# A graph-attention kernel: the four-head aggregation in four 32-column tiles of TensorE instead of two of 64

## The chip, the cores and the metric

The kernel runs on one core of one Trainium2 chip. The metric is the device time of one execution, in microseconds (us). The kernel before took 2711.55 us, the median of two runs (2709.53 and 2713.56 us). The profile that is read here is of one execution whose span is 2711.9 us.

## The reference

Four layers of graph attention follow one another on 16 independent graphs of 1024 nodes with 256 features each. All graphs share one 1024 x 1024 adjacency matrix, which is thin and symmetric and has ones on its diagonal. Layers 0 and 2 have four heads of 64 features, layers 1 and 3 one head of 256. Cut to its core, a layer is:

```python
h = relu(layernorm(x))                       # per node, over 256 features
Wh = h @ W                                   # (1024, 256) @ (256, 256), split into H heads of D
e = leaky_relu(a_src . Wh_i + a_dst . Wh_j)  # one number for each pair (i, j) and head
alpha = softmax over j of e, where adj[i, j] is set
x = x + elu(alpha @ Wh)                      # layer 3: relu in place of elu
```

All of it is in float32. The large piece of arithmetic is `alpha @ Wh`: for each of the 64 pairs of graph and layer, a 1024 x 1024 matrix of weights for each head, times the projected features.

## The kernel before

The kernel computes unnormalised weights, `w[j, i] = max(grow[i], rcol[j]) * mask[j, i]`, with source nodes j on the partitions and target nodes i along the free dimension, and folds the remaining factor into the projected features `whx`. An extra column of `whx` carries the denominator of the softmax, so a four-head product has 64 + 1 = 65 columns and a one-head product 256 + 1 = 257. There are 8 blocks of 128 nodes (`C = 8`).

```python
def weights(n, h, jc):                       # VectorE: one tile of weights, 128 sources x 1024 targets
    w = state[n]["w", h, jc] = work.tile([P, N], F32, name="w", bufs=WBUFS)       # WBUFS = 18
    nc.vector.scalar_tensor_tensor(w, state[n]["g", h], state[n]["rcol"][:, jc, h:h + 1],
                                   masks[...][:, jc, :], op0=ALU.max, op1=ALU.mult)

def aggregate(n, h, i0, per):                # TensorE: per blocks of 128 targets, from block i0 on
    H = LAYERS[steps[n][1]][0]
    D = F // H
    st = state[n]
    ...
    acc = ps_acc.tile([P, per, D + 1], F32, name="acc")                           # 2 buffers
    cols = P // 2 if H > 1 else P
    for q in range(per):
        for jc in range(C):

            for o in range((i0 + q) * P, (i0 + q + 1) * P, cols):
                nc.tensor.matmul(acc[o % P:o % P + cols, q, :],
                                 lhsT=st["w", h, jc][:, o:o + cols],
                                 rhs=st["whx"][:, jc, h, :], start=(jc == 0),
                                 stop=(jc == C - 1))
    nc.scalar.activation(st["y"][:, i0:i0 + per, h, :], acc, AF.Copy)
```

In `aggregate` the weights `w` are the stationary operand (they are loaded into the array) and `whx` is the moving one (it streams through). A four-head layer calls it with `per = 4` (two groups for each head, so 32 x 4 x 2 = 256 groups), a one-head layer with `per = 1`. With `cols = 64` each block of 128 targets is made by two matmuls: targets 0 to 63 go to the left half of the array's columns and to partitions 0 to 63 of `acc`, targets 64 to 127 to the right half and to partitions 64 to 127. The sum over the eight `jc` is accumulated in PSUM.

The two other users of TensorE that matter are the projection (`pw`, line 233: the transposed features times `wx`) and the transposes ahead of it (line 221). The program interleaves pieces of the preparation of later steps between the groups of `aggregate`; the order is fixed when the program is built.

Of the kernel before, what the change touches and what calls it, by code (L numbers as in the profile page):

```python
# [32 lines left out]
P = 128  # L33
# [24 lines left out]
def kernel(ctx: ExitStack, tc: tile.TileContext, x, adj, ws, avs, out):  # L58
# [234 lines left out]
    def aggregate(n, h, i0, per):  # L293
# [3 lines that stand above are left out]
        if h == 0 and i0 == 0:  # L297
            st["y"] = work.tile([P, C, H, D + 1], F32, name="y")
        acc = ps_acc.tile([P, per, D + 1], F32, name="acc")
        cols = P // 2 if H > 1 else P  # L300
        for q in range(per):
            for jc in range(C):

# [6 lines that stand above are left out]
# [128 lines left out]
    with tc.manual_schedule():  # L438
# [50 lines left out]
        for n in range(len(steps)):  # L489
            for k, (h, i0, per) in enumerate(groups(n)):  # L490
                while planned < len(steps) and agenda_of[planned][0] <= 8 * n + k:
                    plan(planned)
                    planned += 1
                emit_tiles(place[n, h, C - 1] + 1, must=True)
                aggregate(n, h, i0, per)
                if i0 + per == C:
                    done["free"] = place[n, h, C - 1] + 1
                while ending and ending[0][0] <= k:
                    ending.pop(0)[1]()
                if 8 * n + k in later:  # L500
                    later[8 * n + k]()
                prepare(8 * n + k)
                ahead = 6 if per > 1 else 3
                emit_tiles(min(done["tiles"] + ahead, done["free"] + WBUFS))
            for _, piece in ending:
                piece()
            ending = finish(n)
# [35 lines left out]
```

## Time and profile before

| What | Value |
|---|---|
| time | 2711.55 us (2709.53 to 2713.56) |
| span of the profiled execution | 2711.9 us |
| TensorE matmuls busy | 2567.2 us, 95% of the span, 40080 records |
| TensorE weight loads busy | 2269.2 us, 84%, 40080 records |
| VectorE busy | 1900.3 us, 70% |
| ScalarE busy | 1229.6 us, 45% |
| GpSimd busy | 992.3 us, 37% |
| mean granted TensorE clock | 0.984 of full speed |

"PE" is TensorE's matmuls, "PEld" its weight loads, DVE is VectorE, ACT is ScalarE, POOL is GpSimd. A line such as L305 is the line of the kernel that issued the instruction. Matmuls are pipelined, and the end of one is modelled in the profile: the duration of a record holds the latency of the array, and many records overlap. So the busy share of PE says that it nearly always had something in flight, and not how near it is to its limit. How fast a stretch of matmuls goes is read from starts: the time of an unbroken stretch divided by the number of records in it.

Every float32 matmul of `aggregate` and of the projection stands in the trace as two records, each with a weight load of its own: the program's 16384 four-head matmuls are 32768 records. The built program holds, for each such matmul, a weight load and a matmul and then once more a weight load and a matmul, on the same tile of the array. They are called its two passes here.

### The profile page before, as it was taken

The numbers are of one execution on the slowest core, as the hardware profiler recorded it, in microseconds if no ns is written. First come the engines' busy times: TensorE is split into PE (matmuls) and PEld (weight loads), VectorE is DVE, ScalarE is ACT, GpSimd is POOL, SyncE is SP. The second block draws the span as 40 slices with busy tenths as digits, with TensorE's granted clock in tenths as the row PEclk, the third lists the DMA queues.
The fourth block names the chain that finished last, engine by engine and source line by source line (L and its number), as shares of the span: only waits on it lengthen the run. The fifth ranks groups of instructions, "written<-read, shape, count | busy, mean of one in ns | idle before, by whom it ended". The sixth has DMA issues, their size and how long they took to land.

```text
span 2711.9 us, 89498 instructions
## 1 busy us (share of the span) xinstructions
PE 2567.2 (95%) x40080; PEld 2269.2 (84%) x40080; DVE 1900.3 (70%) x2041; ACT 1229.6 (45%) x3337; POOL 992.3 (37%) x1242
## 2 busy tenths in 40 slices
PE   3799999999999999999999999999999999999998
PEld 2688888888888888888888888888888888788876
DVE  3796686477875688666876778748687567678752
ACT  3344445444354554544444454544435444444431
POOL 2133424423424534344242353442332443443321
PEclk9899999999999999999999999999999999999999
DMA  3211011012122011002201211101212110011111
GB/s 117 87 42 45 10 45 41 19 62 66 41 72 71 27 49 41 18 33 72 73 33 49 72 33 42 41 25 57 67 39 72 59 45 18 33 41 42 33 33 55
DMA packets 70846, 130.12 MB, mean 48 GB/s; under 512 B 6208, under 2 KB 49984, under 8 KB 70464
## 3 DMA queue, kind: packets, MB, share of 16 engines
q1 hardware_dynamic: 62144, 120.21, 13.5%
q8 instruction: 316, 5.18, 0.8%
q10 hardware_dynamic: 8320, 4.19, 0.6%
q14 instruction: 66, 0.54, 0.1%
HBM read 106.95 MB, written 17.43 MB: 46 GB/s over the span
## 4 chain that ended last, share of the span: by engine, by line
PE 81%; DVE 8%; ACT 4%; issue 3%; POOL 2%; DMA 1%; ACTq 0%; DVEq 0%; SPq 0%; POOLq 0%
PE acc L305 61%; PE pp L233 16%; DVE w L289 6%; PE pp L221 4%; ACT xn L213 1%; DVE bn L191 1%; DMA w<-in_adj 1%; ACT whx L235 1%; ACT g L284 1%; POOL rstd L204 0%; ACT e L339 0%; POOL y L330 0%; ACT whx L239 0%; PE pp L260 0%; DMA x<-in_x 0%
## 5 line engine op out<-in xcount | busy, mean ns | idle before, releaser
L305 PE MATMUL acc<-whx,w 128*64 128x65 f32 x36864 | 1951.0, 242 | 42.0 <-DVE w L289 28.6
L305 PEld LDWEIGHTS acc<-whx,w 128*64 128x64 f32 x36864 | 1766.8, 145 | 225.2 <-issue 70.4
L289 DVE SCALAR_TENSOR_TENSOR w<-g,rcol,mask 128x1024 f32<-128x1024 f32 x1280 | 1544.1, 1273 | 458.3 <-ACT g L284 412.3
L309 ACT ACTIVATE y<-acc 128x260 f32<-128x260 f32 (+1 forms) x512 | 196.8, 384 | 1085.8 <-PE acc L305 1085.0
L233 PE MATMUL pp<-wx,hT 128*128 128x258 f32 (+1 forms) x2048 | 513.2, 394 | 9.0 <-ACT hT L222 7.6
L330 POOL TENSOR_TENSOR y<-y,r 128x1024 f32<-128x1024 f32 x128 | 242.5, 1899 | 594.9 <-DVE r L326 594.9
L233 PEld LDWEIGHTS pp<-wx,hT 128*128 128x128 f32 x2048 | 375.1, 191 | 79.6 <-ACT hT L222 9.9
L346 POOL TENSOR_TENSOR x<-x,e 128x1024 f32<-128x1024 f32 x96 | 226.7, 2366 | 278.0 <-DVE e L345 264.2
L244 POOL TENSOR_TENSOR whx<-whx 128x256 f32<-128x256 f32 x256 | 159.9, 630 | 444.9 <-ACT whx L242 443.5
L213 ACT ACTIVATE xn<-x,shift,rstd 128x256 f32<-128x256 f32 x512 | 264.1, 590 | 126.3 <-POOL shift L207 126.0
L345 DVE SCALAR_TENSOR_TENSOR e<-e,y 128x1024 f32<-128x1024 f32 x96 | 117.6, 1225 | 197.0 <-ACT e L339 197.0
L235 ACT ACTIVATE whx<-pp,nbias 128x4 f32<-128x4 f32 (+1 forms) x512 | 135.0, 264 | 163.1 <-PE pp L233 151.8
L221 PE MATMUL pp<-ident,xn 128*128 128x128 f32 x1024 | 158.0, 287 | 39.0 <-ACT xn L213 28.3
L191 DVE BATCH_NORM_STATS2 bn<-x 128x6 f32<-128x256 f32 x512 | 172.9, 407 | 16.9 <-DMA x<-in_x 14.2
L221 PEld LDWEIGHTS pp<-ident,xn 128*128 128x128 f32 x1024 | 117.3, 144 | 76.7 <-ACT xn L213 36.3
L284 ACT ACTIVATE g<-gs 128x1024 f32<-128x1024 f32 x160 | 162.3, 1018 | 5.3 <-DVE w L289 5.3
L222 ACT ACTIVATE hT<-pp 128x512 f32<-128x512 f32 x256 | 143.2, 592 | 18.5 <-PE pp L221 16.5
L198 POOL TENSOR_TENSOR dev<-bn 128x8 f32<-128x8 f32 x64 | 16.4, 256 | 290.7 <-DVE bn L191 290.7
L239 ACT ACTIVATE whx<-pp,whx 128x256 f32<-128x256 f32 x256 | 121.7, 475 | 0.0
L339 ACT ACTIVATE e<-e 128x1024 f32<-128x1024 f32 x96 | 100.8, 1050 | 33.1 <-POOL e L335 33.1
L204 POOL TENSOR_TENSOR rstd<-rstd,neghalf 128x8 f32<-128x8 f32 x64 | 106.7, 1668 | 5.0
L335 POOL TENSOR_SCALAR e<-y 128x1024 f32<-128x1024 f32 x96 | 100.0, 1042 | 8.5
(45 smaller groups left out, 553.8 us busy)
## 6 DMA issues: line engine op xcount, KB each, us to landing
gs<-grow SPq DMA_DIRECT2D x160, 512.0 KB
x<-in_x SPq DMA_DIRECT2D x16, 1024.0 KB
out<-x SPq DMA_DIRECT2D x32, 512.0 KB
w<-in_adj ACTq DMA_DIRECT2D x8, 512.0 KB
wx<-in_L_gnn_W SPq DMA_DIRECT2D x4, 256.0 KB
e<-in_L_gnn_a SPq DMA_DIRECT2D x8, 128.0 KB
grow<-gT SPq DMA_DIRECT2D x32, 16.0 KB
grow<-gT SPq DMA_DIRECT2D x32, 4.0 KB
```

The costliest lines, as they stand in the source:

```text
L191: nc.vector.bn_stats(bn[:, c, :], xs[b][:, c, :])
L213: nc.scalar.activation(xn[:, q, :], xs[b][:, c, :], AF.Identity, bias=st["shift"][:, c:c + 1], scale=st["rstd"][:, c:c + 1])
L221: nc.tensor.transpose(pt[:, q, :], st["xn", half][:, q, k * P:(k + 1) * P], ident)
L233: nc.tensor.matmul(pw, lhsT=st["hT", half][:, k, q * P:(q + 1) * P], rhs=wx[l][:, k, :], start=(k == 0), stop=(k == K - 1))
L235: nc.scalar.activation(whx[:, c, :, D], pw[:, F + H:F + 2 * H], AF.Exp, bias=nbias[l], scale=slope)
L244: nc.gpsimd.tensor_tensor(whx[:, c, :, 0:D], whx[:, c, :, 0:D], whx[:, c, :, D:D + 1].to_broadcast([P, H, D]), op=ALU.mult)
L284: nc.scalar.activation(g, state[n]["gs", h], AF.Copy)
L289: nc.vector.scalar_tensor_tensor(w, state[n]["g", h], state[n]["rcol"][:, jc, h:h + 1], masks[LAYERS[steps[n][1]][3]][:, jc, :], op0=ALU.m ...
L305: nc.tensor.matmul(acc[o % P:o % P + cols, q, :], lhsT=st["w", h, jc][:, o:o + cols], rhs=st["whx"][:, jc, h, :], start=(jc == 0), stop=(j ...
L309: nc.scalar.activation(st["y"][:, i0:i0 + per, h, :], acc, AF.Copy)
L330: nc.gpsimd.tensor_tensor(yh, yh, r[:, :, None].to_broadcast([P, HALF * H, D]), op=ALU.mult)
L346: nc.gpsimd.tensor_add(xh, xh, e)
```

## The change

One number changes: a block of 128 targets is made by four matmuls on 32 columns of the array each, instead of by two on 64. Each matmul still reads all 65 columns of `whx`; its stationary operand is 32 columns of `w` instead of 64, and its output goes to 32 partitions of `acc` instead of 64. The one-head layers keep their full 128 columns. The idea is that the array then works as four narrow arrays, side by side, whose weight loads are half as long.

```diff
         acc = ps_acc.tile([P, per, D + 1], F32, name="acc")
-        cols = P // 2 if H > 1 else P
+        cols = P // 4 if H > 1 else P
         for q in range(per):
             for jc in range(C):
```

In the order of the built program nothing else moves: the rows of VectorE, ScalarE, GpSimd and the DMA queues are the same, and on TensorE every group of 64 matmuls on 64 columns stands as a group of 128 matmuls on 32 columns at the same place. TensorE's program grows from 40080 pairs of weight load and matmul to 72848.

## The prediction

> **What bounds the kernel now.** I read the page's busy shares first, then the groups by shape, then the chain that ended last, and last the starts of single records.
>
> The groups by shape, matmuls of TensorE alone (busy time, mean of one, idle time before):
>
> ```profile
> L305 PE MATMUL acc<-whx,w 128*64 128x65 f32 x32768 | 1035.1, 225 | 41.2 <-DVE w L289 27.8 <-issue 11.9 <-ACT y L309 0.9
> L305 PE MATMUL acc<-whx,w 128*128 128x257 f32 x4096 | 916.9, 380 | 0.8 <-DVE w L289 0.8
> ```
>
> Only the first row changes. Idle time ahead of it is 41.2 us in the whole run, so these matmuls follow one another nearly without a gap. The chain by line says the same of the kernel as a whole:
>
> ```profile
> PE 81%; DVE 8%; ACT 4%; issue 3%; POOL 2%; DMA 1%; ACTq 0%; DVEq 0%; SPq 0%; POOLq 0%
> ```
>
> TensorE's own work sets the end. Its rate is in the pieces of the chain, start, length, what:
>
> ```profile
> 288.95 7.62 PE acc L305 x256
> 296.77 15.08 PE acc L305 x512
> 328.93 6.96 PE acc L305 x32
> ```
>
> 512 four-head records in 15.08 us are 29.5 ns each; 32 one-head records (257 columns) in 6.96 us are 217.5 ns each. The transposes of line 221, just ahead of the stretch shown next, move 128 columns and start every 109 ns. The two together give (217.5 - 109) / 129 = 0.841 ns a column and 1.3 ns fixed, so 65 columns should take 56.0 ns. A four-head record costs 29.5: two stream at a time, one in each half of the array. The question of this case is what keeps the pair from going faster. Counting the records that have begun at the start of one stretch shows it (the window in us and its length, then busy time with the number of records present in brackets, of matmuls and of weight loads, then clock and DMA; all records begin after 1087.33 and no matmul has ended yet):
>
> ```profile
> 1087.34:1087.35 0.01, 0.01 (x2) 0.01 (x2) 1.00 0.00 0
> 1087.35:1087.43 0.09, 0.09 (x2) 0.09 (x4) 1.00 0.00 0
> 1087.43:1087.45 0.02, 0.02 (x4) 0.02 (x6) 1.00 0.00 0
> 1087.45:1087.49 0.04, 0.04 (x4) 0.04 (x6) 1.00 0.00 0
> 1087.49:1087.51 0.02, 0.02 (x6) 0.02 (x6) 1.00 0.00 0
> ```
>
> Two matmuls begin together, the next two only after 1087.43, the next two after 1087.49. From the first one on, the starts in the trace are 0, 7, 109, 114, 167, 173, 225, 231, 284 ns: pairs 5 to 7 ns apart, a round every 58.3 ns once it runs. The first round is late because it waits for its weights: its records last 272 ns, later ones 222, so a load of 64 columns that nothing hides costs 50 ns. After that, loads run beside the matmuls.
>
> Two things follow. As a tile's two passes stand one behind the other in the program, two matmuls that start together must be of different tiles: the array takes the second tile's first pass ahead of the first tile's second. And a round lasts 58.3 ns, only 2.3 above the 56.0 that 65 columns need. **The stage is bound by streaming**, not by weights, and both halves stream all the time.
>
> **What the Trainium skill says.** "TensorE: Matmul & The Clock Gate", The mechanism (of packing): matmuls on different tiles of the array overlap, about 4 ns apart in start. The trace agrees in kind, with 5 to 7 ns; but the page also says matmuls start strictly in program order, which the pairs here contradict. Same page, LDWEIGHTS (loading the stationary operand): the time goes with the number of columns loaded. That supports halving the 50 ns; no run here shows 32 columns in this place. Same page, Wait — 56ns, not 53.3ns?: start to start never falls below about 25 ns however few the columns. Starts 5 to 7 ns apart on different tiles show that it is no limit across tiles. "TensorEngine Tiling (Array Packing)", Instruction Overhead: don't take the tiling factor from a dimension that is already small. The moving operand is the short one here, but it isn't what is cut.
>
> **The change part by part.**
>
> 1. Streaming: nothing is won. One block of 128 targets with one `jc` is now two rounds (two passes, both halves at once): 2 x 58.3 = 117 ns, times 32 steps x 4 heads x 8 x 8 = 8192 such units = 955 us. With four tiles all four stream the same 65 columns at once, again two passes: two rounds of some 56 ns at least. A quarter of the array's columns does a quarter of the work; the total is the same. If all four run side by side and the round keeps its 58.3 ns: 0 us.
> 2. Overhead of a round: 2.3 ns above what the fit gives. Perhaps the load of 64 columns, at 50 ns nearly as long as the matmul, holds the round up by a nanosecond; then a load of 32 frees it: 16384 rounds x 1 ns = -16 us. With four starts in a round instead of two it may equally grow by 1 to 2 ns: +16 to +33 us. I take -5.
> 3. First load of a stretch: 50 ns becomes about 25 (estimate from the 50, by columns). The trace has 223 unbroken four-head stretches: 223 x 25 ns = -6 us.
> 4. Issue: each round now needs 8 instructions (4 loads, 4 matmuls) in 58 ns, 7.3 ns each, against 14.6 before. What can TensorE's queue deliver? The trace bounds it. Where a semaphore instruction stands ahead of each 8 instructions (at 85.2 us), these instructions start every 125 to 126 ns and each takes 51; the 8 between passed in 75 ns, at most 9.3 ns each. And after a semaphore instruction with an empty queue (at 1011.1 us) a weight load starts, its matmul 31 ns later, and the matmul of the second tile, 4 instructions further on, 6 to 7 ns after that. So the queue delivers 4 instructions in under 7 ns in a burst; sustained it is known only to be below 9.3. I take it as not binding, with a doubt.
> 5. Semaphore instructions on TensorE's queue stay 761 in the built program. They are hidden where the queue has slack, and where one stands ahead of each unit the slack shrinks: before, 126 ns for a unit against 117. With 16 instructions between two of them, up to 76 + 16 x 7.3 = 193 ns if issue is near its bound, else still about 126. Some 470 follow their forerunner by 8: 0 to +31 us. I take +5.
> 6. Other engines: nothing. The evictions, the weights of VectorE (1273 ns each) and the buffers see the same groups at the same times.
>
> Sum: 0 - 5 - 6 + 5, so about -6 us for the wished-for case, before any doubt.
>
> **The rivals.**
>
> *Issue becomes the bound.* If the queue sustains no better than 9.3 ns an instruction, a round takes 74 ns, a unit 148: 8192 x 31 = +254 us, of which up to 28 us are taken from waits for VectorE: about 2940 us. For it: the instructions double while the streaming time stays; the bound in point 4 leaves room. Against: the burst of 4 in under 7 ns.
>
> *Only two tiles ever run at once.* If the array can look past one tile's second pass but not past three tiles' (it must reach 12 instructions ahead), four tiles run as two pairs: a unit takes four rounds, +955 us, 3650 us. Against: at 1013.6 us a semaphore instruction that is 200 instructions behind the last has begun when 164 have, so the queue holds some 36 at least. I give it a few per cent.
>
> *Instruction fetch.* The page has 316 packets of instructions, 5.18 MB, for TensorE's 80921 instructions: 256 in each. At 14.6 ns an instruction one packet is used up in 3.7 us, at 7.3 ns in 1.9 us. In the trace a packet takes 0.9 to 1.4 us, at most 2.0, and they never start less than 3.35 us apart, so how fast they can follow isn't shown. It would bite in the longest stretches only: 0 to +50 us.
>
> *Weight loads were the bound after all.* Loads and matmuls of a round differ by a few ns only. If the loads set the 58.3, halving them gives at best 56.0: 16384 x 2.3 = -38 us, with the first loads -44, 2668 us. That is the most the change can bring; the 95% busy PE doesn't show more to be had.
>
> **Range and chances.** The wished-for case is 2706 us (2711.6 less 6), and most of the doubt lies above it: issue or fetch with about one chance in three, from +20 to +250 us. So 2712 as the middle, 2675 to 2950 for eight in ten. Faster by over 2% needs -54 us, more than even the last rival gives: 0.05. Within 2%: 0.58. Slower: 0.37.
>
> **What would show it.** Right: the four-head row has 65536 records on 128*32; in a stretch of the chain one costs about 14.6 ns (512 of them in 7.5 us); starts come in fours within 25 ns and the fours 57 to 60 ns apart; the first round is 25 ns less late; 217.5 ns stay for one-head records. Issue as the bound: starts spread evenly, 18 ns apart, no fours, with VectorE's waits gone from ahead of the row. Pairs only: 29 ns a record still. Fetch: gaps every 256 instructions. The prediction fails if a record costs over 16 ns in unbroken stretches, or if loads turn out to have been the bound.

## The result, and the profile after

The changed kernel takes 3248.56 us (3246.78 and 3250.34 in two runs) against 2711.55: 1.1977 times the time before, 95% interval 1.1949 to 1.2006. That is 537 us more, where 2712 us and a range of 2675 to 2950 us had been predicted.

First the row that changed, from the groups by shape of the kernel after:

```profile
L305 PE MATMUL acc<-whx,w 128*32 128x65 f32 x65536 | 1102.6, 225 | 504.6 <-issue 495.3 <-DVE w L289 8.5 <-DVE top L140 0.5
L305 PE MATMUL acc<-whx,w 128*128 128x257 f32 x4096 | 917.8, 380 | 0.8 <-DVE w L289 0.8
```

There are 65536 records, as there should be. But the idle time ahead of them is 504.6 us where it was 41.2, and nearly all of it goes to "issue": TensorE waited for nothing that the profile shows. The wait for VectorE, which was most of it before, has shrunk from 27.8 us to 8.5. The one-head row is what it was. The chain, by engine:

```profile
PE 77%; issue 16%; DVE 3%; ACT 2%; DMA 1%; POOL 1%; ACTq 0%; DVEq 0%; SPq 0%; POOLq 0%
```

"Issue" was 3% of 2711.9 us, 81 us; it is now 16% of 3248.6, some 520 us.

Next the start of one stretch of the kernel after (window, busy time and records present of matmuls and of weight loads, clock, DMA; the first matmul begins at 1715.765):

```profile
1715.79:1715.84 0.05, 0.05 (x4) 0.05 (x8) 1.00 0.00 0
1715.84:1715.87 0.03, 0.03 (x8) 0.03 (x12) 1.00 0.00 0
1715.87:1715.90 0.03, 0.03 (x8) 0.03 (x11) 1.00 0.00 0
1715.90:1715.93 0.03, 0.03 (x12) 0.03 (x12) 1.00 0.00 0
```

Matmuls come in fours. Their starts in the trace are 0, 7, 13, 20, then 81, 88, 94, 101, then 138, 145, 151, 158 ns: a round every 56.7 ns. So the array does run four tiles side by side, and even a little faster than two (58.3). The time is lost between such stretches. Pieces of the chain that follow this start and precede it, in order (start, length, what):

```profile
1706.72 3.06 PE acc L305 x203
1709.78 1.61 issue
1711.39 0.99 PE acc L305 x53
1712.38 1.96 PE pp L233 x8
...
1715.84 2.78 PE acc L305 x185
1718.62 1.35 issue
1719.97 1.22 PE acc L305 x71
1721.19 1.94 PE pp L233 x8
1723.14 2.67 PE acc L305 x177
1725.81 1.11 issue
```

A stretch runs at full speed, stops for more than a microsecond in the middle of an accumulation, and goes on. From the first stop to the second there are 53 + 185 four-head matmuls, 8 of the projection and 8 transposes (four of them are in the chain): 254 with as many weight loads, and 4 semaphore instructions, 512 in all. From the second to the third it is 71 + 177 + 8 = 256 pairs, again 512. That is twice 256: 256 instructions after each stop (1716.55 and 1723.74 us in the trace) TensorE goes on without a gap; these 256 hold eight matmuls of the projection and took 5.2 and 3.8 us. Counting TensorE's records from the start of the trace, 354 of its gaps over 0.25 us, from start to start, stand where the count leaves the remainder 193 when divided by 256; they sum to 586.7 us. In the kernel before, 14 gaps stand there, with 16.1 us. The page's line for the instruction queue gives the size of that block, 9.37 MB in 572 packets of 16 KB for 146457 instructions, 256 in each. Here it is, with that of the kernel before under it:

```profile
q8 instruction: 572, 9.37, 1.2%
q8 instruction: 316, 5.18, 0.8%
```

Where a gap of this kind is over 0.6 us (336 of them), the next packet starts 1.14 us after TensorE has gone on (median), the transfer takes 0.99 us, and TensorE goes on 1.39 us after its end: 3.5 us from block to block. In no run of this case do two instruction packets start less than 3.2 us apart; a tenth of the distances in the kernel after are under 3.41 us and a quarter under 3.49. No two packets overlap: one block is on its way at a time.

So the theory, **fetch**: TensorE's program arrives in blocks of 256 instructions, and where TensorE has to wait for each, a block takes about 3.45 us. Two tiles use up a block in 256 x 14.6 ns = 3.7 us, just above; four tiles in 256 x 7.1 ns = 1.8 us. As a sum over the blocks of the built program, with the time that the array needs for each block (7.1 ns an instruction with four tiles, 14.6 with two, half of 217.5 ns for a one-head record, and so on) and the difference to 3.45 us counted where the block is shorter, the kernel before waits 0 us and the kernel after 546 us. The first fits the 16 us of stops counted there, the second the 587.

The rivals are: **array** (four narrow tiles disturb one another beyond what the clean rounds show), **count** (the loss goes with the number of instructions or of bytes, wherever they stand), and **share** (it goes with the number of four-tile matmuls).

### The profile page after: what moved, and what is told of

Its sections match the earlier page's. It is cut to its first block, busy times and chain, and to the rows that moved or that the text cites. A ratio compares the mean times of both kernels' runs of the same rounds, so it can differ in the third digit from the quotient of the medians.

```text
span 3248.6 us, 155034 instructions
## 1 busy us (share of the span) xinstructions
PE 2643.4 (81%) x72848; PEld 2287.4 (70%) x72848; DVE 1913.9 (59%) x2041; ACT 1234.3 (38%) x3337; POOL 985.8 (30%) x1242
## 3 DMA queue, kind: packets, MB, share of 16 engines
q8 instruction: 572, 9.37, 1.2%
## 4 chain that ended last, share of the span: by engine, by line
PE 77%; issue 16%; DVE 3%; ACT 2%; DMA 1%; POOL 1%; ACTq 0%; DVEq 0%; SPq 0%; POOLq 0%
PE acc L305 58%; PE pp L233 14%; PE pp L221 4%; DVE w L289 2%; DMA w<-in_adj 1%; DVE bn L191 0%; ACT whx L235 0%; ACT xn L213 0%; PE pp L260 0%; ACT whx L239 0%; DMA x<-in_x 0%; ACT e L339 0%; ACT whx L242 0%; ACTq L155 0%; ACT g L284 0%
## 5 line engine op out<-in xcount | busy, mean ns | idle before, releaser
L305 PE MATMUL acc<-whx,w 128*32 128x65 f32 x69632 | 2019.3, 234 | 505.4 <-issue 495.3
L305 PEld LDWEIGHTS acc<-whx,w 128*32 128x32 f32 x69632 | 1777.2, 117 | 741.8 <-issue 605.8
L345 DVE SCALAR_TENSOR_TENSOR e<-e,y 128x1024 f32<-128x1024 f32 x96 | 124.2, 1294 | 234.5 <-ACT e L339 234.5
L221 PEld LDWEIGHTS pp<-ident,xn 128*128 128x128 f32 x1024 | 124.9, 152 | 66.9 <-ACT xn L213 24.2
L326 DVE RECIPROCAL r<-y 128x32 f32<-128x32 f32 (+1 forms) x64 | 17.5, 273 | 190.0 <-ACT y L309 190.0
```

The lines of the kernel that those rows point to most:

```text
L221: nc.tensor.transpose(pt[:, q, :], st["xn", half][:, q, k * P:(k + 1) * P], ident)
L305: nc.tensor.matmul(acc[o % P:o % P + cols, q, :], lhsT=st["w", h, jc][:, o:o + cols], rhs=st["whx"][:, jc, h, :], start=(jc == 0), stop=(j ...
```

## The experiments

The kernel before took 2713.7 us beside the first four runs and 2714.59 us beside the others. "Stops" are gaps over 0.25 us at the remainder 193, counted in each trace as above; the model is the sum over blocks of the theory.

| Kernel | TensorE instructions | packets | waiting by the model, us | stops: number, us | time, us |
|---|---|---|---|---|---|
| before | 80921 | 316 | 0 | 14, 16 | 2711.55 |
| after | 146457 | 572 | 546 | 354, 587 | 3248.56 |
| four tiles, 33 columns streamed | 146486 | 572 | 948 | 407, 851 | 3346.16 |
| one-head layers in four tiles | 105496 | 412 | 0 | 13, 15 | 2753.48 |
| half of the blocks in four tiles | 113689 | 444 | 200 | 157, 152 | 2918.41 |
| one tile of 128 | 48153 | 188 | 0 | 3, 3 | 3494.72 |
| one-head in four tiles, cut in four | 191510 | 748 | 563 | 392, 612 | 3399.94 |
| one-head in four tiles, cut in two | 134168 | 524 | 0 | 33, 26 | 2778.76 |
| a quarter of the blocks in four tiles | 97305 | 380 | 56 | 72, 59 | 2763.28 |
| after, nearly without the gs loads | 146457 | 572 | 546 | 363, 575 | 3223.20 |

**Half of the streaming left out.** Edit to the kernel after, four-head layers only: the matmuls stream columns 32 to 64 of whx, and the first half of y is filled with a copy.

```diff
+        lo = D // 2 if H > 1 else 0
...
-                                     rhs=st["whx"][:, jc, h, :], start=(jc == 0),
+                                     rhs=st["whx"][:, jc, h, lo:], start=(jc == 0),
```

> The changed kernel (four tiles of 32), but the four-head matmuls stream 33 of the 65 columns of whx; the columns left out are filled with a copy, so the output is not the reference's. Fetch theory (TensorE's program comes in blocks of 256 instructions, and a block takes at least 3.45 us however fast the array is): the array's four-head time falls by 446 us, but the blocks stay at 3.45 us, so nearly nothing is won: 3190 to 3230 us, against 3248.6 of the changed kernel; gaps still at every 256th instruction. Array theory (four tiles side by side are limited by streaming or by the array itself): 16384 rounds lose 27 ns each, 2800 us or less.

It took 3346.16 us, 1.2327 times the time before (1.2231 to 1.2424): slower than the kernel after, with half the streaming in these layers. The array theory is out: between the stops the array does go faster, a round every 34 ns (median of the starts) where it was 57, and yet the time grew. The fetch theory has the right sign of the stops (587 us became 851) but missed the time by 116 us or more. The reason is in another row of the page, TensorE's granted clock in tenths; here that of this run:

```profile
PEclk8758779988699897899788988899969989897999
```

Its mean is 0.868, against 0.975 in the kernel after. The projection, which the edit doesn't touch, shows the price:

```profile
L233 PE MATMUL pp<-wx,hT 128*128 128x258 f32 x1024 | 318.1, 464 | 4.6 <-ACT y L312 2.1 <-issue 2.0 <-ACT whx L239 0.5
L233 PE MATMUL pp<-wx,hT 128*128 128x264 f32 x1024 | 310.8, 455 | 14.1 <-issue 9.5 <-ACT hT L222 3.2 <-ACT whx L242 1.2
```

These two rows are 255.2 and 259.9 us in the kernel after, so 114 us more here. Two pieces of this run's chain tie it to the clock:

```profile
1701.90 1.98 PE pp L233 x8
1709.51 3.22 PE pp L233 x8
```

In the first the granted clock is 1.00, in the second 0.62. The one-head row and the transposes are 14 and 15 us longer as well. Without these 143 us some 3200 would be left, inside the expected range; that is a sum, not a measurement. The Trainium skill, "TensorE: Matmul & The Clock Gate", What's actually happening, says that TensorE's clock is released by activity and falls back without it. With TensorE busy 74% of the span (81% in the kernel after) that fits; no run here varied the activity alone, so it is an explanation and not shown.

**Four tiles where instructions are few for the time.** Edit to the kernel before:

```diff
-        cols = P // 2 if H > 1 else P
+        cols = P // 2 if H > 1 else P // 4
```

> Four-head layers as before (two tiles of 64), one-head layers in four tiles of 32 instead of one of 128; all of the work is done. TensorE's program grows from 80921 to 105496 instructions. Fetch theory: in a one-head stretch 8 instructions go in 217 ns, a block of 256 in 7 us, far over 3.45 us: 2712 to 2735 us. Array theory (four tiles conflict, as the changed kernel's records went from 29.5 ns a pair to 49): one-head stretches slow down by half or more, 3100 us or more.

2753.48 us, 1.0144 (1.0115 to 1.0173), some 18 us over the top of what was expected and far from 3100. Pieces of the chain, first one-head groups in four tiles, then four-head groups in two:

```profile
236.65 7.10 PE acc L305 x128
...
299.80 15.08 PE acc L305 x512
```

128 records in 7.10 us are 222 ns for a round of four, where one record took 217.5. The difference stands at the edges. Inside, rounds start 216 ns apart (median) in both kernels: four tiles stream 257 columns each, side by side, at the cost of one. But from the last round of an unbroken run to the next matmul it is 327 ns instead of 216, and from the matmul ahead of a run to its first one 214 instead of 152 (medians; the means grow by 107 and 86 ns). There are 152 such runs, so this makes 29 of the 40 us: a change from one shape of tile to another costs about 0.1 us here. The other 11 us were not taken apart.

**Half and a quarter.** Edit to the kernel before (for a quarter, `q == 0`):

```diff
         for q in range(per):
+            cols = (P // 4 if q % 2 == 0 else P // 2) if H > 1 else P
             for jc in range(C):
```

> Four-head layers: of every four blocks of 128 targets two are made in four tiles of 32, two in two tiles of 64. TensorE has 113689 instructions. Fetch theory, block by block over the built program (a block costs the larger of its array time and 3.45 us): 200 us of waiting, 14 us of array time won: 2880 to 2920 us. If the loss goes with the number of four-tile matmuls: half of 537, 2980 us.

> Four-head layers: of every four blocks of 128 targets one is made in four tiles of 32, three in two tiles of 64; 97305 TensorE instructions. Fetch theory, block by block: 56 us of waiting, 7 us won in the array: 2755 to 2785 us. If the loss goes with the share of four-tile matmuls: a quarter of 537, about 2845 us.

2918.41 us (1.0752, 1.0713 to 1.0790) and 2763.28 us (1.0180, 1.0151 to 1.0210). Both are as the blocks predict. The share theory gave 2980 and 2845 us: a quarter of the matmuls costs 49 us, not 134, as a block with only some four-tile matmuls, or with a piece of the projection in it, stays over 3.45 us.

**The other direction.** `cols = P` for all layers:

> Four-head layers in one tile of 128 columns, the other direction of the change; all of the work is done. TensorE has 48153 instructions. If fewer instructions were all that counts, nothing is lost: a pass streams 65 columns in 56 ns, 112 ns a unit against 117, about 2670 us. If the load of 128 columns (109 ns a pass, as in the transposes) sets the pass: 218 ns a unit against 117, 8192 x 101 = +830 us, about 3530 us, without gaps at block ends.

3494.72 us, 1.2875 (1.2833 to 1.2916), with next to no stops at block ends and half the instructions in these layers. A piece of the chain:

```profile
510.58 28.53 PE acc L305 x256
```

That is 111.4 ns a record, twice what 65 columns need for streaming (56.7 ns at most, by the rounds above). A load that nothing hides cost 24 ns for 32 columns (81 less 57) and 50 for 64, so an estimate for 128 is 100. So the load of 128 columns sets the pass. This is what the two tiles of the kernel before are for: 64 columns load in 50 ns, just under the streaming. Fewer instructions alone win nothing.

**Many instructions elsewhere.** One-head layers in four tiles as above, and from `jc = 1` on each matmul cut into four (or, in the other run, two) along the columns; the four-head layers stay in two tiles.

```diff
+                bounds = (0, 65, 129, 193, 257) if H == 1 and jc > 0 else (0, D + 1)
+                for a, e in zip(bounds[:-1], bounds[1:]):
...
-                                     rhs=st["whx"][:, jc, h, :], start=(jc == 0),
+                                         rhs=st["whx"][:, jc, h, a:e], start=(jc == 0),
```

> As the one-head run in four tiles, but from the second jc on each one-head matmul of 257 columns is cut into four of 64 or 65; four-head layers as before. The array's work is the same; TensorE has 191510 instructions, and in a one-head stretch 64 of them for each jc in some 450 ns, 7 ns each. Fetch theory, block by block (at least 3.45 us for 256 instructions): 563 us of waiting at block ends, 40 to 60 us of changes of tile shape and shorter matmuls: 3270 to 3370 us. If the loss belonged to four-head matmuls or to 65-column matmuls with a wait for VectorE behind them: below 2900 us.

> The same with two parts (128 and 129 columns): 134168 TensorE instructions, 92% of the changed kernel's 146457, but spread so that a one-head block of 256 has some 3.5 us of array work. Fetch theory: hardly a block falls under 3.45 us; 2755 to 2810 us (the four-tile one-head run without the cut took 2753). If the number of instructions or bytes as a whole made the loss: 53247 more than before, against 65536 more in the changed kernel, so 81% of 537 us: about 3145 us.

Cut in four: 3399.94 us, 1.2526 (1.2490 to 1.2562). The loss has moved to layers that the change never touched. Rows of this run:

```profile
L307 PE MATMUL acc<-whx,w 128*64 128x65 f32 x32768 | 1032.4, 224 | 38.7 <-DVE w L289 25.7 <-issue 10.5 <-ACT y L311 1.4
L307 PE MATMUL acc<-whx,w 128*32 128x64 f32 x43008 | 945.3, 223 | 376.4 <-issue 375.9
L307 PE MATMUL acc<-whx,w 128*32 128x65 f32 x14336 | 650.6, 224 | 111.9 <-issue 111.8
```

The four-head row is that of the kernel before; the one-head rows now wait 376 and 112 us for "issue". It ended 30 us above the expected range, 80 above its middle; 49 of these are stops (612 us where the model has 563).

Cut in two: 2778.76 us, 1.0237 (1.0208 to 1.0267), within what was expected. This run is the sharpest one. It has 92% of the instructions of the kernel after and loses 64 us instead of 537, 40 of which the run without the cut lost too. In its one-head stretches 128 matmuls, a block with their loads, take 3.74 us by their starts (some 3.5 had been expected), and the cut one-head rows wait 4.1 and 5.5 us, where those cut in four waited 376 and 112:

```profile
L307 PE MATMUL acc<-whx,w 128*32 128x129 f32 x14336 | 743.8, 273 | 4.1 <-issue 4.0
L307 PE MATMUL acc<-whx,w 128*32 128x128 f32 x14336 | 739.5, 272 | 5.5 <-issue 5.4
```

The count theory, which gave 3145 us, is out.

**Is the 3.45 us a matter of sharing the DMA engines?** Edit to the kernel after: gs (one row of factors for all targets, spread over the 128 partitions, 512 KB a load) is loaded twice and then used by all heads, 158 of 160 loads are left out.

> The changed kernel with 158 of the 160 loads of gs left out (all heads use the rows of the first two, so the output is not the reference's): 81 MB of 120 MB of data transfers are gone. If the 3.45 us of a block are the latency of a fetch by itself: 3200 to 3250 us, and the same least distance of the fetches. If they come from sharing the DMA engines with data: the distance falls by half a us or more, 3130 us or less.

3223.20 us, 1.1875 (1.1839 to 1.1910). The waits for "issue" (total, times, longest), first of the kernel after:

```profile
PEld acc L305 <- issue: 605.8, 535, 5.8
```

and of this run:

```profile
PEld acc L309 <- issue: 592.8, 545, 3.5
```

With two thirds of the data transfers gone, the number of waits stays and a tenth of the distances between packets are under 3.44 us (3.41 with the loads): sharing with these loads doesn't set the block's time. What the 3.45 us are made of inside was not taken apart. Only the stops over 4 us go away (8 of them, 39 us together, and none here), so these came from the loads. The sum of all stops falls by 12 us and the time by 25.

## Why the prediction was wrong

- *Point 1, streaming: right.* Four tiles stream side by side, a round takes 56.7 ns (57 to 60 had been named as the sign), and the total of the array's work doesn't change.
- *Point 2, overhead of a round: right in kind.* It fell by 1.6 ns in the stretches shown, 16384 x 1.6 = 26 us won, where 5 were taken. That the load of 64 columns held the round up fits this; no run shows it.
- *Point 3, the first load: right.* The second round begins 81 ns after the first instead of 109.
- *Point 4, issue: this step failed.* It asked what TensorE's queue can take in a burst, found 4 instructions in under 7 ns, and set the sustained rate at "below 9.3 ns". Both are true of the 256 instructions that are there (7.1 ns each). What it took for the sustained rate was the rate inside a block; over many blocks the rate is that of the fetch, 3.45 us / 256 = 13.5 ns an instruction, and the kernel before, with 14.6 ns, was within 8% of it.
- *The rival instruction fetch had the mechanism; its size was off by ten.* It noted that packets never start less than 3.35 us apart and concluded that the limit "isn't shown", since the kernel before never asks for more. It then put the cost at 0 to +50 us "in the longest stretches only", as if many blocks lay ready. Set beside the 1.9 us in which four tiles use a block up, the same 3.35 us read as a latency give the answer: 256 blocks more, and up to 1.6 us for each short one. The Trainium skill has the matter under "Runtime: NRT & Kernel Launch", Instruction fetch mechanics: blocks of 16 KiB, the next one fetched while the present one runs, the cost mostly hidden. The trace agrees with the blocks and not with "mostly hidden".
- *Issue as the bound* named evenly spread starts, 18 ns apart, as its sign. They were not there; the fours were. *Only two tiles at once* and *weight loads were the bound* are out as well, the latter but for the 26 us. (The sum for two tiles, 2712 + 955, is 3667 us and not 3650.)
- *Points 5 and 6* were right as far as seen: the busy times of VectorE, ScalarE and GpSimd are within 14 us of those before. Two semaphore instructions with 16 others between them start 125 ns apart (median of 97), as they did with 8 between, so no cost of theirs shows.
- The sign named for fetch, "gaps every 256 instructions", is what the profile shows.

The terms: 571 us more stops at block ends, 26 won in the rounds, 6 in first loads, give +539 us; measured +537. That is closer than the terms allow, for smaller changes beside it (20 us less waiting for VectorE, a mean clock of 0.975 instead of 0.984) were not taken apart.

No version came out that beats the kernel before. Four tiles win 3.2 ns for each block of 128 targets and `jc`, but need 8 instructions more, 108 ns of fetch. A version that uses four tiles only in blocks with many projection matmuls was not run.

## What to carry to other kernels

Splitting matmuls doubles instructions, and instructions have a price that no engine's busy time shows: divide the array time of an unbroken stretch by its instructions, and where that falls below 13.5 ns (256 instructions in 3.45 us), the fetch sets the time. It is local: cutting the one-head matmuls in two added 28672 well-spread instructions for 25 us, a quarter of the four-head blocks in four tiles added 16384 dense ones for 49 us, cutting in four 86014 dense ones for 647 us. So count by blocks of the program and not in total. And read the least distance between instruction packets in the profile before. By itself it is only an upper bound for the floor (in the run with one tile of 128 it is 11.4 us), but where dense stretches use a block up in little more than that, as here in 3.7 us against 3.35, expect no room for more instructions in them.

## What had not been expected

- A block of TensorE's program takes about 3.45 us where TensorE waits for it (3.2 us is the least distance of two packets in any run): 1.14 us until the fetch starts, 0.99 us of transfer, 1.39 us until TensorE goes on, one block at a time. Leaving out 158 of 160 large loads doesn't shorten it.
- Half of the streaming made the kernel slower, 3346 us against 3249, with 264 us more of stops and the granted clock at 0.868. That the stops lowered the clock was not shown by itself.
- Matmuls on different column tiles seem to start out of program order: with two tiles in pairs, with four in fours 6 to 7 ns apart, though the two passes of a tile stand one behind the other in the program. The records don't name the tile; it is inferred from the starts.
- Four column tiles on 257 columns are as fast as one on all 128: 216 ns from round to round in both. What costs is the change between the two shapes, about 0.1 us each time.
